# Attention over kept tokens: the short output rows share a PSUM bank with values and mean, the short gather becomes 128 rows turned by products, one sum of tokens and some first loads change their slots

## The chip, the cores and the metric

One core of a Trainium2 chip runs the kernel. The metric is device time in microseconds, the median of several executions. Inputs and outputs lie in HBM; the core has on-chip SBUF (128 partitions), eight PSUM banks for matmul results, and five engines with a queue each: TensorE (PE, its weight loads listed as PEld), VectorE (DVE), ScalarE (ACT), GpSimd (POOL) and SyncE (SP), which here only issues transfers.

## The reference

It is a residual attention block over x of shape (8, 512, 1024): batch, features D, tokens T. A mask `cond_2048` keeps about half of the tokens of each batch. Queries, keys and values are one projection, with 8 heads of 64 features.

```python
xt = jnp.transpose(x, (0, 2, 1))
q = xt @ Wq.T
qh = q.reshape(B, T, NH, dk).transpose(0, 2, 1, 3)
scores = scale * jnp.einsum('bhqd,bhkd->bhqk', qh, qh)
logits = (scores * cmask + (1.0 - cmask) * NEG) * rmask
attn = jax.nn.softmax(logits, axis=-1)
ctx = jnp.einsum('bhqk,bhkd->bhqd', attn, qh)
out = ctx.transpose(0, 2, 1, 3).reshape(B, T, D) @ Wo.T
x = x + jnp.transpose(out, (0, 2, 1))
```

A masked key gets no weight. A masked query has only zero logits, so its attention is the plain mean over all tokens: all masked tokens of a batch share one output row.

## The kernel before

It computes attention for the kept tokens alone. A batch has 544 columns (NK): its kept tokens, padded, and in the last column the mean token. They are handled as five blocks (NC = 5): four of 128 columns and a short one (LAST, index 4) of 32. Data is float32 throughout.

**Loops.** The main part (`late`) runs over 32 pairs, p = 0 to 31: batch b = 0 to 7 and pr = 0 to 3, two heads each. A pair has five slots, k = 0 to 4, one for each block of keys, the short block first (`order`). A slot issues scores on TensorE (line 685; 16 matmuls as the trace counts them, or 8 for the short block at line 707) and exponentials on ScalarE (line 693), and then the tasks that `slots_of(p)` put down for it. Everything is in the order written by hand: each engine runs its queue in that order, and waits on semaphores where data or a buffer isn't ready.

**PSUM.** Scores use two tiles of two banks (tag s). Two banks have tag a, two have tag t; `bank(name)` takes the one that was released first. Whoever takes a bank waits until its last reader is through.

**The third pair of a batch (pr = 2).** In it the next batch is prepared, for b = 1 to 6 in this way:
- Slot 1, `mean_with_values`: values of the next pair are transposed (`turn_values`, line 627) into one bank, and their short end into columns of a second bank, which also takes the mean token (`put_mean`, line 572, 16 columns). ScalarE copies the values (`copy_values`, lines 633 and 634), VectorE the mean (line 583).
- Slot 2, `end_attend`: 32 matmuls of contexts (line 749).
- Slot 3: `collect` transposes the five gathered blocks of the next batch (line 558), then `output(b - 1, LAST)` multiplies the 32 short rows of the previous batch's contexts with Wo (line 889, 32 matmuls in the trace), ScalarE copies them (line 898) and GpSimd stores them in four pieces (line 900). Then come two of the seven half-size products (`product`, line 959) that make up the rest of the previous batch's output, and both halves of the next batch's first projection (line 599).

**The seven products** replace the eight of a block-wise product of tokens and Wo, with sums of tokens formed on VectorE (`combine_tokens`, lines 929 to 935) and sums of weights formed once. At pr = 1 the products 1, 6, 7 and 5 run in slot 3; product 7 reads the third sum. Results are added on VectorE (lines 983 to 998).

**Gathering.** x of a batch is transposed to token rows in HBM (`turn`: VectorE line 475, stored by SP line 483). `search` finds, from the rank of each token (line 533, VectorE), which row belongs into which column. `gather` (line 545) fetches the rows by an indirect transfer from GpSimd's queue. `load_piece` (line 388) and `load_ranks` (line 521) load x and ranks two batches ahead, through SP's queue, which also carries `row` and `rb` (lines 845 and 850), the inverse sums of a pair on their way to all partitions. `finish_blocks` (line 1065) transposes finished output rows on VectorE. `queries_of` (line 402, called part in the trace) makes a small mask of the next batch on GpSimd.

Of the kernel before, what the change touches and what calls it, by code (L numbers as in the profile page):

```python
# [306 lines left out]
def attention_of_kept_tokens(ctx, tc, n, x, mask, wq, wo, out, ident, wqT, woT, verdict, flag):  # L307


    nc = tc.nc  # L310
    B, D, T = x.shape
    P = 128
# [11 lines left out]
    LAST = NC - 1  # L324
# [4 lines left out]
    sizes, places = [], []  # L329
# [208 lines left out]
        )  # L538

    def gather(b, i):  # L540
        n = sizes[i]
        if i == 0:
            xins[b] = []
        xin = sb.tile([P, D], F32, tag="xin", name=f"xin_{b}_{i}", bufs=NC)
        nc.gpsimd.indirect_dma_start(  # L545
            out=xin[:n, :],
            out_offset=None,
            in_=xds[b],
            in_offset=bass.IndirectOffsetOnAxis(ap=searches[b][2][:n, i : i + 1], axis=0),
        )  # L550
        xins[b].append(xin)

    def collect(b, i, copy=None, tag="t"):
        n = sizes[i]
        xin = xins[b][i]
        pt = bank(f"xc_{b}_{i}", tag)
        for d in range(ND):
            nc.tensor.transpose(
                pt[:, d * n : (d + 1) * n], xin[:n, d * P : (d + 1) * P], ident[:n, :n]
            )  # L560
        m = min(n, NK - 1 - i * P)
        (copy or nc.scalar.copy)(
            xcs[b][:, :, i * P : i * P + m],
            pt[:, : ND * n].rearrange("p (d n) -> p d n", d=ND)[:, :, :m],
        )
# [309 lines left out]
    def new_rows(b, i, w):  # L875
        if i == LAST and in_halves:
            return sb.tile([P, w], F32, tag="ol", name=f"ol_{b}", bufs=1)
        return sb.tile([P, D], F32, tag="oc", name=f"oc_{b}_{i}", bufs=LAST if in_halves else NC)

    def output(b, i):  # L880
        n = sizes[i]
        if i == 0:
            ods[b] = dr.tile([NK, D], F32, tag="od", name=f"od_{b}")
        po = bank(f"po_{b}_{i}")
        parts = P // n
        w = D // parts
        for pr in range(ND):
            for k in range(parts):
                nc.tensor.matmul(
                    po[k * n : (k + 1) * n, :w],  # L890
                    cTs[b, pr][:, i * P : i * P + n],
                    woT[:, pr, k * w : (k + 1) * w],
                    start=(pr == 0),
                    stop=(pr == ND - 1),
                )

        oc = new_rows(b, i, w)
        nc.scalar.copy(oc[:, :w], po[:, :w])  # L898
        for k in range(parts):
            nc.gpsimd.dma_start(ods[b][places[i], k * w : (k + 1) * w], oc[k * n : (k + 1) * n, :w])  # L900

    HALF = D // 2
    both = {}
# [222 lines left out]
    def slots_of(p):  # L1126

        b, pr = pairs[p]
        todo = [[] for _ in range(NC)]
        before = pairs[p - 1] if 0 < p < len(pairs) - 1 else None  # L1130
        behind = pairs[p + 1] if p + 1 < len(pairs) else None
        ahead = pairs[p + 2] if p + 2 < len(pairs) else None

        def do(k, f, *args):
            todo[k].append(lambda: f(*args))

        late = p == 2
        new = pr == 2 and b + 1 < B
        by_vector = nc.vector.tensor_copy

        def project_with_values():
            project(ahead, 0, lambda end: turn_values(behind, end))
            copy_values(behind)

        def mean_with_values():
            pt = bank(f"mean_{b + 1}")
            turn_values(behind, pt[:, KH : KH + P])
            put_mean(b + 1, pt, lambda: copy_values(behind))

        def project_with_top(hf, tag="t"):  # L1150
            project(ahead, hf, lambda to: turn_top(behind, to), tag)
            bias_of(behind)

        if before:
            do(0, go_on_attend, before)
        due = []
        if pr == 1 and b + 1 == B and in_halves:
            for k, i in ((1, 1), (1, 2), (2, 3), (3, 4)):
                do(k, combine_tokens, b - 1, i)
        elif pr == 1 and b + 1 == B:  # L1160
            due = [1, 2]
            do(2, output, b - 1, 0)
        elif pr > 0 and 0 < b < B - 1 and not in_halves:
            due = {1: (0, 1, LAST), 2: (2,), 3: (3,)}[pr]
        halves = ()
        if in_halves and 0 < b < B - 1:
            halves = ((), (1, 6, 7, 5), (2, 3), (4,))[pr]
            if pr == 1:
                for k, i in ((1, 1), (1, 2), (2, 3), (4, 4)):
                    do(k, combine_tokens, b - 1, i)  # L1170
        if not new:
            if halves and pr == 1:
                leads[p] = [lambda: product(b - 1, 1)]
                halves = halves[1:]
            for i in halves:
                do(3, product, b - 1, i)
            for i in due:
                do(3, output, b - 1, i)
        if in_halves and p == ND:
            do(0, combine_weights)  # L1180
        if p == 0:
            do(0, project, behind, 1)
            do(1, values, behind)
            do(1, lengths_of, behind)
            do(1, project, ahead, 0)
            do(2, project, ahead, 1)
            do(3, bias_of, behind)
        elif late:
            do(1, values, behind)
            do(2, lengths_of, behind)  # L1190
            do(2, end_attend, before)
            do(2, put_mean, b + 1)
            do(2, collect, b + 1, 0)
            do(3, bias_of, behind)
            do(3, collect, b + 1, 1, by_vector, "a")
            do(3, collect, b + 1, 2, None, "a")
            do(4, collect, b + 1, 3)
            do(4, collect, b + 1, 4)
            for hf in range(2):
                do(4, project, ahead, hf, None, "a")  # L1200
        elif new:
            do(1, mean_with_values)
            do(2, end_attend, before)
            do(3, collect, b + 1, 0, by_vector)
            do(3, collect, b + 1, 1, by_vector)
            do(3, collect, b + 1, 2, by_vector, "a")
            do(3, collect, b + 1, 3, None, "a")
            do(3, collect, b + 1, 4, by_vector)
            do(3, lengths_of, behind)
            if halves:  # L1210
                do(3, output, b - 1, LAST)
            for i in halves:
                do(3, product, b - 1, i)
            for i in due:
                do(3, output, b - 1, i)
            do(3, project_with_top, 0)
            do(3, project, ahead, 1, None, "a")
        elif ahead:
            do(1, project_with_values)
            do(2, lengths_of, behind)  # L1220
            do(2, end_attend, before)
            if pr == 1 and b + 1 == B and in_halves:
                for k, i in ((2, 1), (2, 6), (3, 7), (3, 5), (4, 2), (4, 3), (4, 4)):
                    do(k, product, b - 1, i)
            do(3, project_with_top, 1, "a" if halves and pr == 1 else "t")
        elif behind:
            do(1, values, behind)
            do(2, lengths_of, behind)
            do(2, end_attend, before)
            do(3, bias_of, behind)  # L1230
        if p == ND - 1:
            for d in range(ND):
                do(3 + d // 2, turn_weights, woT, "wo", d, None, "at"[d // 2], True)
        if pr == 1 and b + 1 == B:
            if not in_halves:
                do(4, output, b - 1, LAST - 1)
            do(4, output, b - 1, LAST)
        if p + 1 == len(pairs):
            for i in range(NC):
                do((1, 2, 3, 4, 4)[i], begin_output, b, i)  # L1240
        return todo
# [165 lines left out]
    def late(n):  # L1407
# [20 lines left out]

        TURN = [(3, 1), (3, 3), (3, 4), (0, 1)]
        LOAD = {(1, 3): (0, 1), (1, 4): (2, 3, 4, 5), (2, 0): (6, 7)}  # L1430
        TURN_LATER = [(0, 2), (0, 4), (1, 0), (1, 1)]
        SEARCH = {(2, 3): (0,), (2, 4): (1, 2), (3, 3): (3, 4)}
        LATER = {(1, 1): (0,), (1, 2): (1,), (1, 3): (2, 3), (1, 4): (4,)}
# [19 lines left out]
        for p, pair in enumerate(pairs):  # L1453
# [3 lines left out]
            for k, c in enumerate(order):  # L1457
# [45 lines left out]
                if b + 2 < B:  # L1503
                    if pr == 3 and (pr, k) in TURN:
                        turn(b + 2, TURN.index((pr, k)))
                    for i in LOAD.get((pr, k), ()):
                        load_piece(b + 2, i)
                    if pr == 1 and k == 4:
                        load_ranks(b + 2)
                    for i in SEARCH.get((pr, k), ()):  # L1510
                        search(b + 2, i)
# [147 lines left out]
```

## Time and profile before

| what | value |
|---|---|
| median of 3 runs | 636.48 us (633.68 to 638.65) |
| the profiled execution | 635.72 us |
| its span | 634.0 us |
| its granted TensorE clock, mean | 0.985 of full speed |
| data moved | 116.64 MB, mean 184 GB/s |

Times in the profile's rows count from the span's start. A row of a timeline gives the start, the time from the first start to the last end of a run of like instructions, the engine, the line of the kernel, the operation, output and inputs, the shape and the count; in brackets stands the idle time of that engine before it and what ended it. A float matmul that multiplies shows as two instructions, a transpose as one, and each has a weight load of its own in the rows of PEld.

The profiled batch that is looked at most closely below is batch 3; its third pair runs from about 274 to 296 us, and its pairs follow each other in 13 to 22 us.

### The profile page before, as it was taken

The numbers are of one execution on the slowest core, as the hardware profiler recorded it, in microseconds if no ns is written. First come the engines' busy times: TensorE is split into PE (matmuls) and PEld (weight loads), VectorE is DVE, ScalarE is ACT, GpSimd is POOL, SyncE is SP. The second block draws the span as 40 slices with busy tenths as digits, with TensorE's granted clock in tenths as the row PEclk, the third lists the DMA queues.
The fourth block names the chain that finished last, engine by engine and source line by source line (L and its number), as shares of the span: only waits on it lengthen the run. The fifth ranks groups of instructions, "written<-read, shape, count | busy, mean of one in ns | idle before, by whom it ended". The sixth has DMA issues, their size and how long they took to land. (4 is left out here: it accounts for less than half of the span.)

```text
span 634.0 us, 16384 instructions
## 1 busy us (share of the span) xinstructions
PE 602.2 (95%) x6270; PEld 413.6 (65%) x6270; DVE 409.4 (65%) x1139; ACT 366.7 (58%) x983; POOL 225.1 (36%) x317
## 2 busy tenths in 40 slices
PE   5699999999999999999999999999999999999964
PEld 4566576677667766667667766667667766675432
DVE  5539847556568767776568767776568634953643
ACT  4256758754766567753866467753776466526400
POOL 6440403232076204722166205722176204336121
PEclk9999999999999999999999999999999999999985
DMA  6675732355599668977588768878595564696657
GB/s 212 193 234 134 232 109 69 99 199 158 157 178 223 199 209 206 187 238 249 167 178 217 230 207 193 192 223 259 169 184 149 137 210 89 133 300 110 133 178 216
DMA packets 94689, 116.64 MB, mean 184 GB/s; under 512 B 11959, under 2 KB 61815, under 8 KB 94606
## 3 DMA queue, kind: packets, MB, share of 16 engines
q1 hardware_dynamic: 74078, 75.17, 40.6%
q0 software_dynamic: 16208, 38.25, 25.8%
q10 hardware_dynamic: 4320, 2.13, 1.1%
q8 instruction: 50, 0.82, 0.5%
q14 instruction: 33, 0.27, 0.1%
HBM read 72.81 MB, written 42.70 MB: 182 GB/s over the span
## 5 line engine op out<-in xcount | busy, mean ns | idle before, releaser
L693 ACT ACTIVATE e<-s,bias 128x544 f32<-128x544 f32 x256 | 180.7, 711 | 69.4 <-PE s L685 67.1
L685 PE MATMUL s<-qT 64*64 64x272 f32 x2048 | 154.6, 397 | 2.1 <-ACT e L693 1.1
L749 PE MATMUL av<-e,v 64*64 64x272 f32 x1920 | 132.2, 390 | 0.0
L599 PE MATMUL pq<-xc,wqT 128*128 128x272 f32 x512 | 130.8, 400 | 0.0
L599 PEld LDWEIGHTS pq<-xc,wqT 128*128 128x128 f32 x512 | 93.8, 190 | 30.4 <-issue 10.7
L685 PEld LDWEIGHTS s<-qT 64*64 64x64 f32 x2048 | 77.0, 132 | 51.5 <-issue 13.5
L1095 POOL DMA_INDIRECT g<-od,block_origin x56 | 91.1, 1628 | 29.7 <-issue 12.4
L749 PEld LDWEIGHTS av<-e,v 64*64 64x64 f32 x1920 | 77.7, 133 | 36.0 <-issue 0.7
L609 ACT COPY qT<-pq 128x272 f32<-128x272 f32 x64 | 24.6, 384 | 107.3 <-PE pq L656 66.9
L973 POOL DMA_DIRECT2D od<-c x28 | 21.0, 751 | 138.4 <-DVE c L997 81.9
L1065 DVE STREAM_TRANSPOSE xr<-g 128x512 f32<-128x512 f32 x56 | 56.8, 1096 | 0.0
L646 DVE TENSOR_REDUCE len<-sq 128x10 f32<-128x640 f32 x32 | 25.9, 808 | 46.6 <-ACT sq L644 46.6
L693 ACT ACTIVATION_READ_ACCUMULATOR e<-s,bias 128x1 f32 x256 | 50.5, 197 | 0.0
L1092 POOL COPY step<-e 1x1 f32<-1x1 f32 x77 | 28.3, 368 | 53.3 <-ACT e L693 53.0
L545 POOL DMA_INDIRECT xin<-xd,source x40 | 39.0, 974 | 16.4 <-DMA woT<-in_L_cond_Wq_dram 5.8
L900 POOL DMA_DIRECT2D od<-ol x28 | 14.5, 524 | 72.1 <-ACT ol L898 71.2
L959 PE MATMUL po<-t,st 128*128 128x256 f32 x168 | 38.9, 384 | 0.4 <-DVE st L933 0.3
L665 DVE TENSOR_REDUCE m<-pq 128x1 f32<-128x128 f32 x28 | 8.2, 292 | 46.1 <-ACT qT L611 36.1
L959 PEld LDWEIGHTS po<-t,st 128*128 128x128 f32 x168 | 31.1, 190 | 7.0 <-issue 2.2
L475 DVE STREAM_TRANSPOSE xt<-x 128x1024 f32<-128x1024 f32 x28 | 34.8, 1241 | 1.3 <-DMA xd<-xt 0.7
L533 DVE TENSOR_SCALAR_CACHE_REDUCE junk<-rank,key 128x1024 f32<-128x1024 f32 (+4 forms) x35 | 34.9, 998 | 0.0
L494 ACT ACTIVATE junka<-x 128x512 f32<-128x512 f32 x48 | 30.2, 630 | 1.1
(205 smaller groups left out, 844.8 us busy)
## 6 DMA issues: line engine op xcount, KB each, us to landing
xd<-xt SPq DMA_DIRECT2D x120, 128.0 KB
x<-in_x_dram SPq DMA_DIRECT2D x56, 256.0 KB
g<-xd SPq DMA_DIRECT2D x56, 256.0 KB
out_dram<-xr SPq DMA_DIRECT2D x28, 512.0 KB
rb<-row SPq DMA_DIRECT2D x60, 160.0 KB
od<-c POOLq DMA_DIRECT2D x28, 256.0 KB, 6.0
rank<-ranks SPq DMA_DIRECT2D x6, 512.0 KB
x<-in_x_dram POOLq DMA_DIRECT2D x8, 256.0 KB, 6.3
```

The costliest lines, as they stand in the source:

```text
L475: nc.vector.transpose(xt.rearrange("p k (d f) -> p k d f", d=ND), xs[b][r][:, :, at : at + n].rearrange("p d (k t) -> p k d t", t=Q),)
L494: nc.scalar.activation(junk, xs[b][r][:, d, :], AF.Copy, accum_out=xbars[b][:, d, r : r + 1])
L533: nc.vector.tensor_scalar(junk[:, :n], rank[:, i * P :], key[:, col], 0.0, ALU.is_le, ALU.add, accum_out=found[:, col])
L545: nc.gpsimd.indirect_dma_start(out=xin[:n, :], out_offset=None, in_=xds[b], in_offset=bass.IndirectOffsetOnAxis(ap=searches[b][2][:n, i : ...
L599: nc.tensor.matmul(pq[:, :KH], wqT[:, d, pr * P : (pr + 1) * P], xcs[b][:, d, cols], start=(d == 0), stop=(d == ND - 1),)
L685: nc.tensor.matmul(ss[h][r * DK : (r + 1) * DK, hf, :KH], qT[heads[h], c * P + r * DK : c * P + (r + 1) * DK], qT[heads[h], queries[hf]], ...
L693: nc.scalar.activation(e[:, :, h, :], ss[h][:, :, :KH], AF.Exp, bias=bias, scale=SCALE, accum_out=sums[pair[1] % 2][:, h, c : c + 1],)
L749: nc.tensor.matmul(avs[pair][hf][head, :KH], v[keys, c, head], e[keys, hf, h, :], start=(c == 0 and not crossed), stop=(c == LAST - 1 and ...
L959: nc.tensor.matmul(po[:, m * HALF : (m + 1) * HALF], tokens(j, m), features(j), start=(j == 0), stop=(j == 1),)
L1065: nc.vector.transpose(xr.rearrange("p (d a) (t i) -> p a d t i", a=A, i=NT)[..., i], gs[b, i].rearrange("p (a d f) -> p a d f", a=A, f=Q),)
L1092: nc.gpsimd.tensor_copy(step, es[pair, c][0:1, 0, 0, 0:1])
L1095: nc.gpsimd.indirect_dma_start(out=gs[b, i], out_offset=None, in_=ods[b], in_offset=bass.IndirectOffsetOnAxis(ap=block_origin[:, b, i : i ...
```

## The change

Four edits:
1. In pairs with pr = 2 of batches 1 to 6, `output(b - 1, LAST)` moves from slot 3 to slot 1. Its 32 matmuls now stand ahead of the value transposes, its bank takes the short end of the values and the mean as well (columns 128 to 255, and from 256), and ScalarE copies the short rows ahead of the values. On GpSimd the four stores of these rows come ahead of `part`.
2. For all batches but the first, the short gather fetches 128 rows, not 32, and `collect` turns them by matmuls: the 128 gathered rows are the weights, and the first 32 columns of the identity are what moves.
3. In the second pair of batches 1 to 6, the third sum of tokens goes from slot 2 to slot 1. On VectorE it comes ahead of two output transposes.
4. During batch 0, the eight pieces of x of batch 2 go from slots 3 and 4 of pr = 1 and slot 0 of pr = 2 to slots 2 and 3 of pr = 2, and the ranks of batch 2 from slot 4 of pr = 1 to slot 1 of pr = 2. On SP's queue they now come behind the `row` and `rb` of pair 1.

No instruction is added or dropped but for the matmuls that take the place of transposes; the engines' queues are otherwise in the same order.

```diff
     def gather(b, i):
-        n = sizes[i]
+        n = sizes[i] if b == 0 else P
...
         for d in range(ND):
-            nc.tensor.transpose(
-                pt[:, d * n : (d + 1) * n], xin[:n, d * P : (d + 1) * P], ident[:n, :n]
-            )
+            to, cols = pt[:, d * n : (d + 1) * n], slice(d * P, (d + 1) * P)
+            if n == P or b == 0:
+                nc.tensor.transpose(to, xin[:n, cols], ident[:n, :n])
+            else:
+                nc.tensor.matmul(to, xin[:, cols], ident[:, :n], start=True, stop=True)
...
-        oc = new_rows(b, i, w)
-        nc.scalar.copy(oc[:, :w], po[:, :w])
-        for k in range(parts):
-            nc.gpsimd.dma_start(ods[b][places[i], k * w : (k + 1) * w], oc[k * n : (k + 1) * n, :w])
+        def keep_rows():
+            oc = new_rows(b, i, w)
+            nc.scalar.copy(oc[:, :w], po[:, :w])
+            for k in range(parts):
+                rows = oc[k * n : (k + 1) * n, :w]
+                nc.gpsimd.dma_start(ods[b][places[i], k * w : (k + 1) * w], rows)
+
+        if beside:
+            beside(po[:, w:], keep_rows)
+        else:
+            keep_rows()
...
+        def short_with_values():
+            def beside(rest, keep_rows):
+                def copies():
+                    keep_rows()
+                    copy_values(behind)
+
+                turn_values(behind, rest[:, :P])
+                put_mean(b + 1, rest[:, P:], copies)
+
+            output(b - 1, LAST, beside)
...
-                for k, i in ((1, 1), (1, 2), (2, 3), (4, 4)):
+                for k, i in ((1, 1), (1, 2), (1, 3), (4, 4)):
                     do(k, combine_tokens, b - 1, i)
...
-            do(1, mean_with_values)
+            do(1, short_with_values if halves else mean_with_values)
...
-            if halves:
-                do(3, output, b - 1, LAST)
...
+        LOAD_LATER = {(2, 2): (0, 1, 2, 3), (2, 3): (4, 5, 6, 7)}
...
-                    for i in LOAD.get((pr, k), ()):
+                    for i in (LOAD if b else LOAD_LATER).get((pr, k), ()):
                         load_piece(b + 2, i)
-                    if pr == 1 and k == 4:
+                    if (pr, k) == ((1, 4) if b else (2, 1)):
                         load_ranks(b + 2)
```

More of the change, by code (lines that the diff above doesn't have):

```diff
@@ L878, in new_rows, with output @@
         return sb.tile([P, D], F32, tag="oc", name=f"oc_{b}_{i}", bufs=LAST if in_halves else NC)
-    def output(b, i):
+    def output(b, i, beside=None):
         n = sizes[i]
```

## The prediction

> **What bounds the kernel now.** I read the page's span and busy times first, then who TensorE waited for, then the order of instructions around the places that the change touches, engine by engine.
>
> ```profile
> span 634.0 us, 16384 instructions
> PE 602.2 (95%) x6270; PEld 413.6 (65%) x6270; DVE 409.4 (65%) x1139; ACT 366.7 (58%) x983; POOL 225.1 (36%) x317
> ```
>
> TensorE (PE) is busy for 95% of the span, so only what shortens or fills its queue counts. The view of PE's waits names hardly any, and one that this change touches:
>
> ```profile
> PE po L959 <- DVE st L933: 0.3, 2, 0.2
> ```
>
> That list hides more than it shows, because a stalled matmul is modelled as busy. So I went through batch 3's third pair (pr = 2) by start times. The rows of PE matmuls, with a stretch of an ordinary pair below for comparison:
>
> ```profile
> 279.92 0.29 PE L572 MATMUL mean<-mean,within 128*128 128x16 f32 x2
> 280.33 1.60 PE L685 MATMUL s<-qT 64*64 64x272 f32 x14
> ...
> 284.85 2.48 PE L558 MATMUL xc<-ident,xin 128*128 128x128 f32 x20
> ...
> 303.28 1.15 PE L685 MATMUL s<-qT 64*64 64x272 f32 x16
> ...
> 307.11 1.99 PE L959 MATMUL po<-t,cT 128*128 128x256 f32 x8
> ```
>
> Both stretches are 16 score matmuls, 32 context matmuls, 16 score matmuls, then something of another tile size. The ordinary one takes 307.11 - 303.28 = 3.83 us; this one takes 284.85 - 280.33 = 4.52. So 0.69 us are lost in slots 1 and 2. The weight loads say where, columns being start, length, group and the idle time before it:
>
> ```profile
> 279.81 0.30 PEld L572 LDWEIGHTS mean<-mean,within 128*128 128x128 f32 x2
> 280.33 0.20 PEld L685 LDWEIGHTS s<-qT 64*64 64x64 f32 x4 [0.22 <-ACT e L693]
> 281.03 0.42 PEld L685 LDWEIGHTS s<-qT 64*64 64x64 f32 x10 [0.50 <-ACT e L693]
> ...
> 285.43 1.29 PEld L558 LDWEIGHTS xc<-ident,xin 128*128 128x128 f32 x12 [0.17 <-DVE xc L583]
> 286.89 0.32 PEld L558 LDWEIGHTS xc<-ident,xin 32*128 32x128 f32 x4 [0.17 <-DVE xc L562]
> 287.25 0.81 PEld L889 LDWEIGHTS po<-woT,cT 128*32 128x32 f32 x32
> 288.26 1.59 PEld L959 LDWEIGHTS po<-woT,cT 128*128 128x128 f32 x8 [0.20 <-issue]
> ```
>
> Slot 1 has too little for TensorE: values and mean are done at 280.21, and the next scores stand until ScalarE's two exponentials give back the score banks (0.22, then 0.50). Slot 3, where the short output sits (287.25), has no such hole.
>
> **Part 1: short output into slot 1 (batches 1 to 6, six times).** Its 32 matmuls take 288.26 - 287.25 = 1.01 us. Put ahead of the values they start at the point where the values start now; everything behind them comes 1.01 us later. The scores then need no bank that isn't free: without the first wait (0.20 of the 0.22) they would start at 280.33 - 0.20 + 1.01 = 281.14, and the second bank was free at 281.03. So 0.69 + 0.20 = 0.89 of the 1.01 come back, and slots 1 and 2 grow by 0.12. The margin is only 0.11 us.
>
> ScalarE gets the copy of the short rows between its exponentials and the values' copies.
>
> ```profile
> 280.87 0.26 ACT L633 COPY v<-mean 128x128 f32<-128x128 f32 x1
> ...
> 281.85 0.71 ACT L693 ACTIVATE e<-s,bias 128x544 f32<-128x544 f32 x1 [0.23 <-PE s L685]
> ```
>
> A copy of that size is 0.26; ScalarE is idle for 0.23 before the next exponential, and that now comes about half a microsecond later, because its scores do. I cost the copy at nothing; without that cover it is 0.26 x 6 = 1.6 us.
>
> The mean stays in this bank until VectorE reads it, and the second group of transposes (285.43) waits for just that:
>
> ```profile
> 283.88 0.40 DVE L722 CUSTOM_DVE_ANT_0 junk<-el,part 128x272 f32<-128x272 f32 x1
> ...
> 284.69 0.68 DVE L583 TENSOR_SCALAR xc<-mean 32x4 f32<-32x4 f32 x4
> ```
>
> ```profile
>   DVE xc L583: 1.1, 5
> ```
>
> The last row, from the transposes' own list of releasers, sums that wait to 1.1 us in five batches. TensorE arrives 0.12 later, so it would swallow the 0.12, if VectorE keeps its time. But the change also moves GpSimd's work: the four stores of the short rows, now at 288.96, come first, and the two halves of the next batch's query mask (part), which run ahead of them now, queue behind them.
>
> ```profile
> 288.96 2.09 POOL L900 DMA_DIRECT2D od<-ol  x4 [12.50 <-ACT ol L898]
> ...
> 347.85 0.96 POOL L402 TENSOR_SCALAR part<-count,kept 64x272 f32<-64x272 f32 x1 [2.03 <-DMA xin<-xd,source]
> ```
>
> (The second row is one half of part in the next batch.) The copy being done at about 281.2, the stores run to 283.3 and the two halves of part from there to 285.2: right beside the VectorE instructions that lead to the mean. Nobody waits for part, which is the next batch's. What it does to VectorE is the open price: bounds 0 and 1.4 us (second rival); I take 0.15 late per batch, which the wait hands on to TensorE whole: six times 0.15 = +0.9 us for slots 1 and 2 together.
>
> In slot 3 the short output leaves, and with part 2 the tile size no longer changes there. From the start of the last big transpose's load (the twelve end at 286.72, a load is 0.14 long, so 286.58) to the product's first load at 288.26 it is 1.68 us now.
>
> **Part 2: the short gather as products (seven times).** Four transposes of a 32-row tile become four float matmuls with full 128-row weights and 32 moving columns. The trace shows each float matmul as two instructions (the mean is one call and x2 above), so eight. The nearest row is the mean: 128x128 weights, 16 columns, two loads of 0.19 in 0.30, so 0.11 apart; eight take 0.9. Ends: the 32-row loads (four of 0.14 within 0.32: 0.06 apart) give 0.5, loads that do not overlap give 8 x 0.19 = 1.5. I take 0.9, since the mean has the same weights and nearly as little to move. [...]
>
> So slot 3 becomes 0.11 (the last transpose's own step) + 0.9 = 1.01 in place of 1.68: -0.67, six times: -4.0 us. In batch 0 there is no short output to take away; the old short group is 287.25 - 286.58 = 0.67 long, the new one 1.01: +0.34 once.
>
> The gather itself moves 128 rows, not 32:
>
> ```profile
> L545 POOL DMA_INDIRECT xin<-xd,source x40: 872/972/1108, 21.7 to 482.8; - x40
> ```
>
> From the shortest to the longest of all gathers it is 0.24 us of GpSimd, which has just that to do there. The rows are transposed most of a pair later, and the 192 KB more per batch have that time too. Cost nothing; were the short rows late, TensorE would stand for them one for one, and its view of waits has no such entry behind the first batch's start.
>
> **Part 3: third sum a slot sooner.** On VectorE the third sum now runs ahead of two output transposes, not behind them.
>
> ```profile
> 195.82 1.89 PE L959 MATMUL po<-t,st 128*128 128x256 f32 x8
> ...
> 201.51 1.77 PE L599 MATMUL pq<-xc,wqT 128*128 128x272 f32 x7
> ...
> 337.65 5.34 PE L959 MATMUL po<-t,st 128*128 128x256 f32 x24
> 342.83 2.00 PE L599 MATMUL pq<-xc,wqT 128*128 128x272 f32 x8
> ...
> 479.44 5.78 PE L959 MATMUL po<-t,st 128*128 128x256 f32 x24
> 485.06 2.00 PE L599 MATMUL pq<-xc,wqT 128*128 128x272 f32 x8
> ```
>
> ```profile
> 195.46 2.03 DVE L1065 STREAM_TRANSPOSE xr<-g 128x512 f32<-128x512 f32 x2
> ...
> 198.94 0.69 DVE L983 TENSOR_TENSOR c<-po,c 128x512 f32<-128x512 f32 x1
> ```
>
> The 24 matmuls of three products take 342.83 - 337.65 = 5.18 in batch 4, start to start, and 201.51 - 195.82 = 5.69 in batch 2: 0.5 lost. The sum would be 2.03 earlier and no longer late. What is late next is VectorE's addition that frees a bank for the last product: it ends at 199.63, its queue being as long as before, so that product starts near 199.7 in place of 200.0 and 0.3 are won. The list of waits counts two such batches; the third (485.06 - 479.44 = 5.62, 0.44 lost) is not in it. Three times 0.27: -0.8 us. Ends: 0 and 1.5.
>
> **Part 4: later loads in batch 0.** Eight loads of x and the ranks move on SP's queue behind the row and rb transfers of pair 1.
>
> ```profile
> 77.78 1.09 SPq L850 DMA_DIRECT2D rb<-row  x2
> ```
>
> ```profile
> 76.90 1.27 DVE L533 TENSOR_SCALAR_CACHE_REDUCE junk<-rank,key 128x1024 f32<-128x1024 f32 x1
> ...
> 82.51 0.23 DVE L860 TENSOR_TENSOR rb<-rb 128x64 f32<-128x64 f32 x1 [1.77 <-DMA rb<-row]
> ...
> 93.30 0.82 DVE L646 TENSOR_REDUCE len<-sq 128x10 f32<-128x640 f32 x1 [5.11 <-ACT sq L644]
> ```
>
> The ranks now leave after rb, at 78.9 at the latest, and land, by rb's own 82.51 - 77.78 = 4.7, at about 83.6 at the latest; the pieces of x follow them. VectorE's search, standing at 76.90, would then start 6.7 late and push what follows by up to 4.8 (1.8 of it were a wait already). Behind it stand three searches, pair 1's contexts, pair 2's inverses and a transpose of x; TensorE needs none of them before the idle 5.11 at 93.30 has absorbed it. Cost nothing; without that cover, one for one. The view of PE's waits names no transfer in this stretch, so nothing is gained either. Ends: -0.5 and +2 us.
>
> **The sum.** -4.0 + 0.9 + 0.34 - 0.8 = -3.6 us (0.6%). The profiled execution took 635.72 us (span 634.0), 0.8 below the median of 636.48; the loop's share of it is the same in any run, so I take the difference off the median: 632.9.
>
> **The rivals.** First, the products are dear: eight loads that do not overlap, 1.5 in place of 0.9, seven times 0.6 = +4.3 us: 637.2, no gain. Against it: the mean's two loads of 0.19 fit in 0.30. Or they are cheap, 0.06 apart: 0.5, so seven times -0.4 = -2.9: 630.0. Against it: that was seen for 32-row transposes alone.
>
> Second, and slower than before: part holds up VectorE in front of the mean. How that looks is seen where GpSimd adds weights:
>
> ```profile
> 103.63 1.12 DVE L860 TENSOR_TENSOR rb<-rb 128x64 f32<-128x64 f32 x1
> ```
>
> ```profile
> 103.40 1.27 POOL L915 TENSOR_TENSOR t<-woT 128x512 f32<-128x512 f32 x1
> ```
>
> The same VectorE instruction takes 0.23 at 82.51 and 1.12 here, to about the end of GpSimd's. If each half of part blocks one of the two-input instructions at 283.88 in that way, they end at 284.7 and 286.1 and the mean is read 1.4 late: 6 x (1.4 - 0.15) = +7.5 us: 640.4. It turns the change into a loss from a lateness of 0.15 + 3.6 / 6 = 0.75 us per batch. Against it stands a two-input addition that ran beside part:
>
> ```profile
> 348.07 0.88 DVE L935 TENSOR_TENSOR st<-cT,st 128x256 f32<-128x256 f32 x2
> ```
>
> ```profile
> L935 DVE TENSOR_TENSOR st<-cT,st x14: 399/412/546, 134.1 to 553.6; 128x256 f32<-128x256 f32 x14
> ```
>
> The pair of additions started within part (347.85 to 348.81) and both were done at 348.95; the slower took 546 ns where the median is 412. That excess is my 0.15. [...]
>
> Third, a gain in one slot is given back in the next, because some bank or exponential that I take to be just in time (margin 0.11) is late: six times 0.5 = +3 us, 636.
>
> **How the numbers follow.** Forecast 0.55 (its own range 631 to 635); dear products 0.13; cheap products 0.12; blocked VectorE 0.10; given back 0.10. Runs of this kernel spread from 633.68 to 638.65, so about 1% (6.4 us) is what can be told from no change. The range 629.5 to 638 holds all but the far side of the cheap case and the blocked one. Faster by over 1% (below 630.1) is half of the cheap case and the low tail of the forecast: 0.14. Slower by over 1% (above 642.8) needs both parts to block in full and more: 0.05. The rest, 0.81, is within 1%.
>
> **What would show it.** Part 1: in pr = 2 no wait of score loads for ACT e behind the mean, and the first transpose 3.8 us after those scores start, not 4.5. Part 2: eight short-gather loads 0.11 apart, no idle time before the products that follow. Part 3: no wait of po for st. Part 4: VectorE waits for the rank transfer near 77 to 83, TensorE does not. The prediction is wrong if the transposes of pr = 2 wait longer for the mean than now, or if the eight loads take over 1.3 us.

## The result and the profile after

| | median | runs | kernel before, same chip |
|---|---|---|---|
| changed kernel | 631.85 us (630.33 to 633.27) | 17 | 634.35 us, 17 runs |

The ratio of the two is 0.9952, with a 95% interval from 0.9938 to 0.9967: 0.3 to 0.6% faster, 2.1 to 3.9 us; the two medians differ by 2.5 us. The forecast was 632.9 us, 3.6 less than before, within 1%. The profiled execution of the changed kernel took 632.33 us. The head of its page:

```profile
span 630.5 us, 16440 instructions
...
PE 597.7 (95%) x6298; PEld 416.8 (66%) x6298; DVE 411.2 (65%) x1139; ACT 367.0 (58%) x983; POOL 223.5 (35%) x317
```

The span is 3.5 us shorter with 56 more instructions: 28 matmuls and their 28 weight loads, four each in seven batches. TensorE's share is still 95%. As before, the place of the change shows only by start times. Batch 3's third pair, TensorE's matmuls (start, length, line, tile size, shape, count):

```profile
277.09 1.08 PE L891 MATMUL po<-woT,cT 128*32 128x128 f32 x32
...
278.93 1.15 PE L687 MATMUL s<-qT 64*64 64x272 f32 x16
...
282.79 2.14 PE L560 MATMUL xc<-ident,xin 128*128 128x128 f32 x16
284.76 0.98 PE L562 MATMUL xc<-ident,xin 128*128 128x32 f32 x8
285.57 1.97 PE L968 MATMUL po<-woT,cT 128*128 128x256 f32 x8
```

From the scores' start to the first transpose it is 282.79 - 278.93 = 3.86 us, like an ordinary pair's 3.83; before it was 4.52. The weight loads of the same stretch, with the idle time ahead of a group in brackets:

```profile
278.10 0.42 PEld L629 LDWEIGHTS v<-ident,qT 128*128 128x128 f32 x4 [0.20 <-issue]
...
278.93 0.67 PEld L687 LDWEIGHTS s<-qT 64*64 64x64 f32 x16
...
282.79 0.42 PEld L560 LDWEIGHTS xc<-ident,xin 128*128 128x128 f32 x4 [0.41 <-DMA od<-ol]
283.39 1.29 PEld L560 LDWEIGHTS xc<-ident,xin 128*128 128x128 f32 x12 [0.19 <-DVE xc L585]
284.65 0.97 PEld L562 LDWEIGHTS xc<-ident,xin 128*128 128x128 f32 x8
285.55 1.60 PEld L968 LDWEIGHTS po<-woT,cT 128*128 128x128 f32 x8
```

The score loads at 278.93 stand in one group: the two waits for ScalarE's exponentials are gone. The 0.41 us ahead of the transposes are not new: the kernel before has them at the same place, put down to "issue".

```profile
284.84 0.42 PEld L558 LDWEIGHTS xc<-ident,xin 128*128 128x128 f32 x4 [0.41 <-issue]
```

The eight loads of the products follow each other in (285.55 - 284.65) / 8 = 0.11 us, with nothing idle behind them. The 0.20 us where the tile changes from the short output's 128x32 to 128x128 moved along with it: they stood ahead of the products at 288.26, and stand ahead of the values now. What came in addition is a longer wait for the mean. The transposes' list of releasers had 1.1 us for it before; now:

```profile
  DVE xc L585: 1.5, 5
```

To see where every part of the 3.5 us went, I took from the timeline of each profiled execution the start of every pair's exponential of the short block (el, one for each of the 32 pairs), and from these the time from one pair to the next. The table shows by how much three stretches were longer than in the shortest of ten kernels that ran on chips where the kernel before takes about 635 us (the experiments are told below). All other stretches between pairs agree within 0.06 us, but for 0.23 in one place (pr = 1 of batch 0, third sum late).

| kernel | pr = 2, batch 0 | pr = 2, batches 1 to 6, sum | pr = 1, batches 1 to 6, sum |
|---|---|---|---|
| before | 0.12 | 6.11 | 1.66 |
| changed | 0.46 | 3.46 | 0.54 |
| part 1 alone | 0.12 | 1.22 | 1.02 |
| without products | 0.12 | 1.40 | 0.42 |
| mask first | 7.77 | 2.51 | 1.12 |
| full turns | 0.00 | 0.53 | 0.48 |
| third sum late | 0.46 | 3.09 | 1.33 |
| loads early | 0.46 | 2.89 | 1.24 |
| mask first from batch 1 | 0.46 | 2.66 | 1.00 |
| full turns and mask | 0.00 | 0.07 | 0.01 |

Changed against before: +0.34, -2.65 and -1.12, together -3.4 us.

### The profile page after: what moved, and what is told of

It is laid out like the page before. It is cut to its first block, busy times and chain, and to the rows that moved or that the text cites. A ratio compares the mean times of both kernels' runs of the same rounds, so it can differ in the third digit from the quotient of the medians.

```text
span 630.5 us, 16440 instructions
## 1 busy us (share of the span) xinstructions
PE 597.7 (95%) x6298; PEld 416.8 (66%) x6298; DVE 411.2 (65%) x1139; ACT 367.0 (58%) x983; POOL 223.5 (35%) x317
## 5 line engine op out<-in xcount | busy, mean ns | idle before, releaser
L687 PE MATMUL s<-qT 64*64 64x272 f32 x2048 | 148.6, 396 | 1.2 <-ACT e L695 1.1
L751 PE MATMUL av<-e,v 64*64 64x272 f32 x1920 | 129.6, 390 | 0.0
L687 PEld LDWEIGHTS s<-qT 64*64 64x64 f32 x2048 | 75.0, 132 | 47.4 <-issue 13.3
L751 PEld LDWEIGHTS av<-e,v 64*64 64x64 f32 x1920 | 76.1, 133 | 36.1 <-issue 0.6
L1101 POOL COPY step<-e 1x1 f32<-1x1 f32 x77 | 26.5, 344 | 55.0 <-ACT e L695 54.7
```

The costliest lines, as they stand in the source:

```text
L687: nc.tensor.matmul(ss[h][r * DK : (r + 1) * DK, hf, :KH], qT[heads[h], c * P + r * DK : c * P + (r + 1) * DK], qT[heads[h], queries[hf]], ...
L751: nc.tensor.matmul(avs[pair][hf][head, :KH], v[keys, c, head], e[keys, hf, h, :], start=(c == 0 and not crossed), stop=(c == LAST - 1 and ...
L1101: nc.gpsimd.tensor_copy(step, es[pair, c][0:1, 0, 0, 0:1])
```

## The experiments

Each kernel computes the whole reference. Ratios are to the kernel before on the same chip, with the 95% interval; the changed kernel's is 0.9952. A difference of 0.001 is 0.63 us.

**Part 1 alone.** The kernel before with this and the functions that it calls:

```diff
-            do(1, mean_with_values)
+            do(1, short_with_values if halves else mean_with_values)
...
-            if halves:
-                do(3, output, b - 1, LAST)
```

> The kernel before with part 1 alone: the short output goes into slot 1 of the pairs pr = 2 of batches 1 to 6 and shares the bank of values and mean; gathers, sums and loads stay as before. My theory is that the tile size now changes only for the four short transposes, and that these stay as dear as they were: slot 3 loses the 1.01 us of the 32 matmuls whole, slots 1 and 2 grow by 0.12 and by the 0.2 us that the mean was seen late in the changed kernel. That is 0.7 us a batch, six times: 4.2 us less than before, range 3.3 to 5.0, so more than the whole change brought (2.5 to 3.1), and no step of +0.33 in batch 0. The rival (the short output's removal brings nothing unless the change of tile size goes too) expects 2 us or less.

629.98 us, ratio 0.9918 (0.9891 to 0.9945): 5.0 us less than before by the medians, 5.2 by the ratio, at the upper end of the range (3.3 to 5.0) or just past it, and more than the whole change brought. In its third pairs 4.89 us went (6.11 to 1.22), 0.8 a batch. The weight loads of slot 3 in batch 3:

```profile
282.65 1.29 PEld L558 LDWEIGHTS xc<-ident,xin 128*128 128x128 f32 x12 [0.18 <-DVE xc L583]
284.12 0.32 PEld L558 LDWEIGHTS xc<-ident,xin 32*128 32x128 f32 x4 [0.17 <-DVE xc L562]
284.48 1.59 PEld L966 LDWEIGHTS po<-woT,cT 128*128 128x128 f32 x8
```

From the second group's first load to the first product it is 284.48 - 282.65 = 1.83 us; in the changed kernel 285.55 - 283.39 = 2.16. The two changes of tile size around the 32-row transposes (0.17 idle ahead of them, 0.04 behind) are cheaper than the products that avoid them. The rival fell.

**Part 2 undone** in the changed kernel:

```diff
-        n = sizes[i] if b == 0 else P
+        n = sizes[i]
...
+            nc.tensor.transpose(
+                pt[:, d * n : (d + 1) * n], xin[:n, d * P : (d + 1) * P], ident[:n, :n]
+            )
```

> The changed kernel with part 2 undone: the short gather fetches its 32 rows and turns them by four transposes of a 32-row tile, as before. My theory, from batch 0, where the products alone were added and the pair came 0.33 us later: the products cost more than the transposes and the two changes of tile size together, in every batch, so this kernel is 7 x 0.33 = 2.3 us faster than the changed one (range 1.5 to 3.0). The rival, on which the prediction's slot 3 rests (the products pay by keeping the tile size), expects it slower than the changed one, by up to 2 us.

629.37 us, ratio 0.9914 (0.9885 to 0.9944), 0.0038 or 2.4 us less than the changed kernel. The table has 0.34 in batch 0 and 2.06 in the six others, 2.4 too. So the products are a loss in every batch, and the gain of slot 3 is all part 1's.

**Full turns.** The gather of 128 rows is kept, but `collect` turns them whole:

```diff
-        n = sizes[i]
+        n = sizes[i] if b == 0 else P
...
+            nc.tensor.transpose(
+                pt[:, d * n : (d + 1) * n], xin[:n, d * P : (d + 1) * P], ident[:n, :n]
+            )
-        m = min(n, NK - 1 - i * P)
+        m = min(sizes[i], NK - 1 - i * P)
```

> The changed kernel, but the 128 gathered rows of the short group are turned by four full 128x128 transposes, as those of the other groups are, in place of products of which only 32 columns are asked for. No change of tile size, and four loads with four matmuls in place of eight with eight. By the spacing of the full transposes, 0.11 us each, four take 0.44 in place of 0.90: 7 x 0.46 = 3.2 us faster than the changed kernel (range 2.3 to 3.6). The rival (the moving columns count as well as the loads: 128 in place of 32 each) expects 1.5 us or less. Beside the kernel with the 32-row transposes it should be 0.5 to 1.0 us faster.

628.18 us, ratio 0.9890 (0.9866 to 0.9915): 3.9 us less than the changed kernel by the ratios, 3.4 by the table's first two columns (0.46 + 2.93); 3.2 was expected (2.3 to 3.6), and the rival's 1.5 or less falls. Beside the kernel with 32-row transposes, on the same chip, it is 1.2 us less by the medians; those two intervals overlap, and the first two columns of the table give 1.0. Batch 3, weight loads of slot 3:

```profile
282.25 1.73 PEld L558 LDWEIGHTS xc<-ident,xin 128*128 128x128 f32 x16 [0.18 <-DVE xc L583]
283.94 1.60 PEld L966 LDWEIGHTS po<-woT,cT 128*128 128x128 f32 x8
```

Sixteen loads and on to the product in 283.94 - 282.25 = 1.69 us, 0.47 less than with products and 0.14 less than with 32-row transposes (1.83). The moving columns (128 for 32) did not show here: what differs in the rows is the count of instructions, one load and one matmul for a transpose where a float product has two of each.

**The mask first.** The next batch's query mask (part) is asked of GpSimd ahead of the stores of the short rows:

```diff
-                    if pr == 2 and k == 2:
+                    if pr == 2 and k == 0:
```

> The changed kernel, with the next batch's query mask (part) asked of GpSimd at the start of slot 0 of pr = 2, ahead of the stores of the short rows, as it ran before; all else as changed. My theory: part then no longer runs beside the VectorE instructions that lead to the mean; the mean is read 0.2 us earlier per batch, and the second group of transposes starts that much earlier: 6 x 0.2 = 1.2 us faster than the changed kernel (range 0.5 to 1.6), with the custom instruction of line 724 back at 0.44 us. Rivals: the stores themselves, now later, hold up something (slower), or the wait for the mean is set by the exponentials and nothing is gained (0).

638.42 us, ratio 1.0052 (1.0029 to 1.0076): 6.3 us more than the changed kernel by the ratios, where 1.2 less was expected. The table puts it in one place, batch 0. GpSimd there:

```profile
71.21 0.97 POOL L402 TENSOR_SCALAR part<-count,kept 64x272 f32<-64x272 f32 x1
74.04 0.96 POOL L402 TENSOR_SCALAR part<-count,kept 64x272 f32<-64x272 f32 x1 [1.86 <-DMA xin<-xd,source]
...
75.40 1.02 POOL L545 DMA_INDIRECT xin<-xd,source  x1 [0.16 <-POOL step L1101]
```

The second half of the mask waits 1.86 us for a transfer, and the last gather of the short rows queues behind it: it is issued at 75.40, in the changed kernel at 71.36. The expectation had asked whom the later stores would hold up, and not what batch 0 has queued behind the mask. TensorE stands for these rows, and then runs slowly:

```profile
81.58 1.54 PE L562 MATMUL xc<-ident,xin 128*128 128x32 f32 x8 [3.73 <-DMA xin<-xd,source]
82.93 6.81 PE L601 MATMUL pq<-xc,wqT 128*128 128x272 f32 x16
```

In the changed kernel the same 16 matmuls take less:

```profile
78.46 3.91 PE L601 MATMUL pq<-xc,wqT 128*128 128x272 f32 x16
```

In the five later batches that have such a mask and a late mean (2 to 6) the step went the way the theory said, 0.95 us less than in the changed kernel where 0.2 for each had been expected; in batch 1 there was nothing to win. So the edit was made again with `k == (0 if b else 2)`.

**A second group on another chip.** The mended edit, parts 3 and 4 undone one at a time, and full turns with the mended mask:

```diff
-                for k, i in ((1, 1), (1, 2), (1, 3), (4, 4)):
+                for k, i in ((1, 1), (1, 2), (2, 3), (4, 4)):
```

```diff
-                    for i in (LOAD if b else LOAD_LATER).get((pr, k), ()):
+                    for i in LOAD.get((pr, k), ()):
...
-                    if (pr, k) == ((1, 4) if b else (2, 1)):
+                    if (pr, k) == (1, 4):
```

> The changed kernel, with the next batch's query mask ahead of the stores of the short rows in batches 1 to 6 alone; in batch 0, where the earlier mask held up the last gather and cost 7.3 us in the run before, it stays where the change has it. My theory: the 7.3 us are gone and what the later batches showed there stays, the sum of the steps of batches 2 to 6: 0.9 us less than the changed kernel (range 0.4 to 1.3). The rival (the loss of that run also sits in the stores being later) expects it slower than the changed one.

> The changed kernel with part 3 undone: the third sum of tokens in slot 2 of pr = 1, behind two output transposes. My theory: the waits of po for st come back in about three batches, with the idle time that the trace showed to go: 1.1 us more than the changed kernel (the prediction had 0.8), range 0.4 to 1.7. The rival, that the pairs' gains there were other chance delays of VectorE, expects 0 and no wait of po for st.

> The changed kernel with part 4 undone: batch 0 loads the second batch's x and ranks in pair 1, as before. My theory: VectorE's wait of 4.9 us for the ranks goes, the idle time before the length reduction grows by as much, and TensorE sees nothing: the same time within 0.5 us. The rivals: the loads were in the way of something of TensorE's (up to 2 us more than the changed kernel), or VectorE's wait did cost (up to 2 us less).

> Full transposes of the 128-row short gather and the mask ahead of the stores from batch 1 on, together. If the two savings sit at different places of slot 3 (the last group of transposes, the second group's wait for the mean) they add up: 3.2 and 0.9 us, 4.1 us less than the changed kernel (range 3.3 to 4.8), about 627.7 us. The rival, that the one hides behind the other, expects no more than the full transposes alone.

Here the kernel before took 646.06 us, and the four, in the order of the expectations, 640.24 (0.9896, 0.9852 to 0.9940), 641.90 (0.9913, 0.9872 to 0.9954), 647.67 (1.0011, 0.9977 to 1.0045) and 641.18 (0.9888, 0.9840 to 0.9937). In all four, batch 0's third pair was 2.3 to 3.5 us longer than in the changed kernel on the other chip, for a reason that was not found, and most pairs with pr = 1 were 0.8 to 4.2 us longer, by amounts that differ from batch to batch and from kernel to kernel, so nothing of 1 us can be read from the times. What stands late there is VectorE's first addition of a product, here in the kernel with the loads early:

```profile
278.61 0.69 DVE L992 TENSOR_TENSOR c<-po,c 128x512 f32<-128x512 f32 x1 [3.55 <-PE po L968]
```

and TensorE behind it, here with the third sum late:

```profile
206.77 1.99 PE L968 MATMUL po<-t,st 128*128 128x256 f32 x8 [2.09 <-DVE c L992]
```

In the first of these two, the last of the matmuls named as releaser had started more than three us earlier (16 from 273.55, 0.22 apart, of which the addition needs the first eight), so the wait is for something else, which the trace does not name; it stays open. The third pairs, free of this, could be read: with the mask first, the pairs behind them came 0.15 to 0.35 us earlier in batches 2 to 6, 1.2 in all; with both edits 0.46 to 0.65 in each of batches 1 to 6.

**The same four again**, on a chip with 635.11 us for the kernel before.

> The kernel of the second group with the third sum back in slot 2, once more: there the chip gave 646 us for the kernel before, with pairs pr = 1 two us longer in most batches of every kernel, so that nothing of this size could be read. On a chip that gives about 635 us for the kernel before: 1.1 us more than the changed kernel (range 0.4 to 1.7), lost in pairs pr = 1 where po waits for st. The rival: 0, and no such wait.

631.33 us, ratio 0.9937 (0.9913 to 0.9961): not slower than the changed kernel. The expectation of +1.1 failed in the times. In the profile it loses 1.33 us in the pairs pr = 1, 0.8 more than the changed one, and the wait is there in one batch (5):

```profile
404.84 1.89 PE L968 MATMUL po<-t,st 128*128 128x256 f32 x8
407.29 3.79 PE L968 MATMUL po<-t,st 128*128 128x256 f32 x16 [0.56 <-DVE st L942]
```

But kernels with the sum early lose there too, by the wait that the prediction had named as next; with the mask first from batch 1, in batch 3:

```profile
264.36 3.65 PE L968 MATMUL po<-t,st 128*128 128x256 f32 x16
268.70 1.99 PE L968 MATMUL po<-t,st 128*128 128x256 f32 x8 [0.69 <-DVE c L992]
```

The last column of the table has 1.0 to 1.7 us for the three kernels with the sum late and 0.0 to 1.2 for the seven with it early (means 1.34 and 0.69), each seen once. A gain of about half a us would fit that; the times do not show it. What does divide the two sorts without exception is the wait itself: a product stands for the third sum in the three kernels with the sum late (0.3 us before, 0.6 in part 1 alone and here) and in none of the seven with it early.

> The kernel of the second group with the loads of batch 0 as before, once more. My theory stays: 0, within 0.5 us, with the pairs of batch 0 the same. The rivals: up to 2 us more than the changed kernel (the loads were in the way), or up to 2 us less (VectorE's wait did cost).

632.39 us, ratio 0.9960 (0.9933 to 0.9986), against 0.9952: no difference. The pairs of batch 0 start at the same distances as in the changed kernel, to 0.02 us. As expected.

> The mask ahead of the stores from batch 1 on, once more. In the second group slot 3 came 0.15 to 0.35 us earlier in batches 2 to 6, 1.2 us in all, with the mean's wait at its 0.49. So 1.0 us less than the changed kernel (range 0.5 to 1.4). The rival: the stores, now later, cost it back: 0 or more.

630.94 us, ratio 0.9940 (0.9913 to 0.9966), 0.8 us less than the changed kernel, where 1.0 was expected (0.5 to 1.4); the intervals overlap. The table has 0.8 less in the third pairs. What happened is plain in batch 4, first in the changed kernel, GpSimd and VectorE:

```profile
349.67 2.01 POOL L904 DMA_DIRECT2D od<-ol  x4 [7.59 <-ACT v L635]
351.71 2.12 POOL L402 TENSOR_SCALAR part<-count,kept 64x272 f32<-64x272 f32 x2
```

```profile
351.85 0.67 DVE L724 CUSTOM_DVE_ANT_0 junk<-el,part 128x272 f32<-128x272 f32 x1
...
352.56 0.44 DVE L724 CUSTOM_DVE_ANT_0 junk<-el,part 128x272 f32<-128x272 f32 x1
```

then with the mask first, the same two engines:

```profile
342.69 0.98 POOL L402 TENSOR_SCALAR part<-count,kept 64x272 f32<-64x272 f32 x1
345.41 0.96 POOL L402 TENSOR_SCALAR part<-count,kept 64x272 f32<-64x272 f32 x1 [1.74 <-DMA xin<-xd,source]
350.23 2.15 POOL L904 DMA_DIRECT2D od<-ol  x4 [3.86 <-ACT v L635]
```

```profile
352.37 0.40 DVE L724 CUSTOM_DVE_ANT_0 junk<-el,part 128x272 f32<-128x272 f32 x1
...
352.81 0.44 DVE L724 CUSTOM_DVE_ANT_0 junk<-el,part 128x272 f32<-128x272 f32 x1
```

The VectorE instruction beside part takes 0.67 us, without it 0.40. In the changed kernel's batch the second group of transposes starts 0.80 us behind the first, and both take 0.80 + 1.29 = 2.09; with the mask first all sixteen run on, in 1.78. Weight loads, changed kernel first:

```profile
352.86 0.42 PEld L560 LDWEIGHTS xc<-ident,xin 128*128 128x128 f32 x4 [0.41 <-DMA od<-ol]
353.66 1.29 PEld L560 LDWEIGHTS xc<-ident,xin 128*128 128x128 f32 x12 [0.38 <-DVE xc L585]
```

```profile
353.43 1.78 PEld L560 LDWEIGHTS xc<-ident,xin 128*128 128x128 f32 x16 [0.41 <-DMA od<-ol]
```

> Full transposes and the mask ahead of the stores from batch 1 on, once more. In the second group the steps of slot 3 were 0.46 to 0.65 us less than the changed kernel's in each of batches 1 to 6, 3.3 in all, but the mean was still seen 0.1 us late. So 3.3 us less than the changed kernel plus 0.46 in batch 0: 3.7 us (range 3.0 to 4.5), about 628 us where the kernel before takes 634.5. The rival: no more than the full transposes alone brought, 3.2.

627.37 us, ratio 0.9876 (0.9837 to 0.9915): the fastest of all, 1.2% less than before. It is 4.8 us less than the changed kernel by the ratios, a little more than was expected (3.0 to 4.5); the table has 4.4. In batch 4 all twenty transposes run through:

```profile
350.98 2.22 PEld L558 LDWEIGHTS xc<-ident,xin 128*128 128x128 f32 x20 [0.41 <-DMA od<-ol]
353.16 1.60 PEld L966 LDWEIGHTS po<-woT,cT 128*128 128x128 f32 x8
```

The two savings add up for the most part, since they sit at different places of the slot: in the third pairs the table has 3.4 for the full turns, 0.8 for the mask and 3.85 for both. The other 0.5 of the table's 4.4 are pairs pr = 1 without any wait in this one execution, which neither edit aims at.

## Why the prediction was right, point by point

- **Slot 1 has too little for TensorE, and the short output fills it: right.** The waits for exponentials went, and the stretch takes 3.86 us as forecast (3.8).
- **Slots 1 and 2 grow by 0.15 a batch: too small.** From the start of slot 1's matmuls (the values before, the short output now) to the first transpose it is 282.79 - 277.09 = 5.70 us in batch 3, where it was 284.85 - 279.31 = 5.54. The start of the values in the kernel before:

```profile
279.31 0.66 PE L627 MATMUL v<-ident,qT 128*128 128x128 f32 x4
```

That is +0.16 in place of the 0.12 that the mean's wait was to swallow. The short output itself took the 1.01 us that it was given (278.10 - 277.09); the rest is 0.83 from the values to the scores for 0.82, and 3.86 behind them for 3.83. The mean's wait did not swallow it; it grew itself, from 1.1 us in five batches to 1.5, 0.07 a batch over six, so VectorE came late by more than TensorE did. Together 0.23 a batch, 1.4 us for 0.9. The prediction had named a longer wait for the mean as a sign that it is wrong, and this sign came. Its own sum already had VectorE 0.15 late and TensorE 0.12, so a wait longer by 0.03: the sign contradicted the sum. The lateness stayed far from the 0.75 a batch at which the change would have been a loss.
- **Slot 3, 1.68 to 1.01 us: right to the hundredth.** 12 loads end at 284.68, a load is 0.14 long, so the last one's start is 284.54, and the product's first is at 285.55: 1.01. Six times -0.67 are -4.0, and -4.0 + 1.4 = -2.6 is the table's -2.65. The working put this down to both edits together. Taken apart, part 1 alone leaves 284.48 - (282.65 + 1.29 - 0.14) = 0.68 of the 1.68, so it gives -1.00, and part 2 takes back 0.33. The prediction's own figures, 0.67 for the old short group and 1.01 for the new one, already said that the products lose in every batch; it drew this for batch 0 alone.
- **Eight loads of the products 0.11 apart, 0.9 us: right**, as was +0.34 in batch 0 (0.46 for 0.12). Both rivals on their price fell. The full turns' loads, with 128 rows too, stand 0.106 us apart (1.69 / 16), and the 32-row loads of part 1 alone 0.06 (four of 0.14 within 0.32), as in the kernel before.
- **The copy on ScalarE is hidden: right.** ScalarE still waits for TensorE behind it:

```profile
280.17 0.71 ACT L695 ACTIVATE e<-s,bias 128x544 f32<-128x544 f32 x1 [0.21 <-PE s L687]
```

- **part beside VectorE: a delay of this size, not a block.** The instructions beside it took up to 0.67 for 0.40 us, and the rival needed them to stand for the whole 0.96 each. The long delay that the prediction read at 103.63 (1.12 for 0.23 us) was beside another instruction on GpSimd, an addition of weights; line 724 has none like it in the changed kernel (at most 0.667 us in 64).
- **Third sum, -0.8: the mechanism was right, the size is not shown.** The profiles gave -1.1 at first, yet the sum put back did not slow the kernel in 12 runs. Which batch waits differs from profile to profile, and a difference of two single profiles was taken for the edit's worth. That the sum early ends the wait for it is borne out by the ten profiles above; what this is worth in time is not. The wait named as late next is there, in batch 5 of the changed kernel, while batch 2 runs through:

```profile
194.79 5.34 PE L968 MATMUL po<-t,st 128*128 128x256 f32 x24
...
409.09 1.99 PE L968 MATMUL po<-t,st 128*128 128x256 f32 x8 [0.26 <-DVE c L992]
```

- **Later loads cost nothing: right.** VectorE waits for the ranks, and the idle time at the length reduction shrinks from 5.11 to 2.33:

```profile
81.00 1.28 DVE L533 TENSOR_SCALAR_CACHE_REDUCE junk<-rank,key 128x1024 f32<-128x1024 f32 x1 [4.88 <-DMA rank<-ranks]
...
92.78 0.82 DVE L648 TENSOR_REDUCE len<-sq 128x10 f32<-128x640 f32 x1 [2.33 <-ACT sq L646]
```

With the loads early the row at 92.72 shows 5.30 again, and the time is the same.

The sum of -3.6 held at -2.5 to -3.0 because its largest term was read from the rows of the place itself; its errors were 0.5 in slots 1 and 2 and up to 0.8 in the third sum. That the time itself came within 1.1 us (631.85 for 632.9) is in part luck: the forecast was taken off a median of three runs, 636.48, and 17 runs of the same kernel gave 634.35. A base 2.1 too high and a saving 1.1 too large partly cancel.

## What to carry to other kernels

A change that bundles edits can hide a loss: here moving work into a hole brought 5 us, and a second edit meant to smooth the same place took half of it back, and the pair in batch 0, where that edit stood alone, showed it. When only a part of a block is needed, count the instructions first: turning the whole block cost less (1.69 us from the second group's first load to the product) than a narrow product (2.16) or a narrow transpose (1.83). Before a task is moved on a queue, look at every batch that uses that slot: the same move that won about 0.2 us in each of five later batches lost 7.3 in the first.

## What the runs showed of the hardware beyond that

In one run a stall of TensorE cost twice its length. In the run with the mask first it stood 3.73 us for the late rows; the granted clock in that stretch, by windows (start to end; length; busy time and count of PE, PEld, DVE, ACT, POOL; clock; DMA share; GB/s):

```profile
78.00:81.00 3.00, 0.00 (x0) 0.00 (x0) 0.00 (x0) 0.86 (x3) 0.00 (x0) 1.00 1.01 297
81.00:82.00 1.00, 0.42 (x4) 0.45 (x5) 0.99 (x1) 0.00 (x0) 0.00 (x0) 0.98 0.90 270
82.00:83.00 1.00, 1.00 (x7) 1.00 (x6) 0.96 (x4) 0.00 (x0) 0.00 (x0) 0.50 1.07 408
...
87.00:88.00 1.00, 1.00 (x3) 0.70 (x3) 0.79 (x6) 0.32 (x1) 0.00 (x0) 0.50 0.00 0
88.00:89.00 1.00, 1.00 (x4) 0.79 (x3) 0.45 (x3) 0.00 (x0) 0.00 (x0) 0.60 0.00 0
89.00:90.00 1.00, 1.00 (x8) 0.46 (x6) 0.00 (x0) 0.23 (x1) 0.00 (x0) 1.00 0.02 3
```

From 82.0 to 88.8 (0.60 in the last mixed row: 0.8 us at half, 0.2 at full) the clock was at half, 6.8 us long, although TensorE had work again from 81.58; the stall of 3.7, the 16 projection matmuls with 6.81 us for 3.91, and the eight products ahead of them with 1.54 for 0.98 come to 7.2 of the 7.3. What these 24 matmuls lost, 2.9 and 0.6, is half of the 6.8. In the stall itself the clock was still full (1.00 from 78 to 81, 0.98 in the row behind), and in the changed kernel, which has no such stall, it is 1.00 in all of 70 to 100. What lowered it at 82.0 and what brought it back at 88.8 this run does not show.
